# A gated graph layer in fp32: the pairwise-distance products in four row groups of TensorE, written ahead of the projection

## The chip, the core and the metric

The kernel runs on one core of a Trainium2 chip. A core has five engines, each with its own queue of instructions that it works through in order: TensorE (matrix products, in the profile PE, with its weight loads as PEld), VectorE (DVE), ScalarE (ACT), GpSimd (POOL) and SyncE (SP), which issues transfers. An engine waits for another through semaphores. SBUF is the working memory; TensorE writes its products to PSUM, which has eight banks, and VectorE or ScalarE reads them from there. The metric is the device time of one execution in microseconds. Three runs of the kernel before took 2278.29, 2275.20 and 2278.82 us; the median is 2278.29 us. The profile is of one further execution of 2278.09 us, whose span is 2276.3 us.

## The reference

There are 64 graphs of 256 nodes with 256 features each, all in fp32. Cut to what matters for one graph `x` with adjacency `adj`:

```
h      = relu(bn(conv1(x)))                  # 1x1 convolution
x_conv = relu(bn(conv2(h)) + x)              # 17 taps along the nodes
s      = x @ w_se.T + b_se                   # 256 nodes x 3 coordinates
dist   = |s_n|^2 + |s_m|^2 - 2 s_n . s_m     # 256 x 256
A      = exp(-dist) * adj
x_nmp  = A @ relu(x @ w_msg.T + b_msg)
r, z, n = GRU gates of ([x_conv, x_nmp], x)  # 512 -> 768 and 256 -> 768
x1     = layernorm(x + (1 - z) * n + z * x)
out    = layernorm(x1 + layer 1 of (x1, adj))
```

Layer 1 normalizes x1, aggregates it over `adj`, multiplies by two weights (W_rel, W_root), takes the relu, adds x1, and the result is normalized again. The change touches only how `dist` is computed and when. The matrix of distances is symmetric, and its rank is small: the product that makes it contracts over 4 values a node, three coordinates and a norm.

## The kernel before, in words

A graph's 256 nodes are two halves of 128, since SBUF and TensorE have 128 rows; `C` is 2. All products are fp32, which TensorE does in two passes, so that a product has two weight loads and two matmul records in the profile (transposes have one).

The main loop goes over 8 batches of 8 graphs. In iteration `k` it does, for different graphs at once, the stages of a software pipeline: the gates of graph `k` (`gates_rz`, `gates_n`, once for each half), the message passing of `k + 1` (`passing`), the factors and the distances of `k + 2` (`factors`, `distances`), the messages of `k + 3` (`messages`), and the projection and aggregation of `k - 1` (`transposes_h`, `project`, `aggregate`). Between the stages stand calls of `pump()`, each of which emits a slice of the convolution of the next batch. The convolution is done by a tree of splits on VectorE (the many instructions at L103, L302, L304, L361, L431 on the tile XF), products on TensorE (L384) and merges on VectorE. In the first part of a batch `pump()` instead emits conv1: transposes of x (L456), their copy by ScalarE (L457), the product (L465) and its activation (L481). The last batch has no convolution to prepare.

The order of the work on every engine is the order in which it is written (`manual_schedule`): nothing is moved by a planner. So where a stage is written sets what stands behind it on each of the engines.

The PSUM pool has eight banks under one tag. A bank comes back when the last reader of its tile has been written, and the banks are given out again in the order in which they came back. The first product into a bank waits until the earlier tile's reader has run.

The path of the distances of a graph, in the lines that the prediction speaks of:

- `messages` (L637): the product with the message weights also gives the 3 coordinates of a node. VectorE (L652) writes them into a tile `st`, twice, 32 columns apart (SR = 32), and GpSimd writes the norm beside each (L663). L654 adds the bias of the messages.
- `factors` (L667): TensorE transposes `st` (L671), so that the two copies come to rows 0 to 3 and 32 to 35 (ROWS = 36); ScalarE makes the two factors `lr` of it (L673, L674).
- `distances` (L677): one product for each half of the rows, 4 rows deep and 256 columns wide, each from its own copy: the products sit in two different groups of 32 rows of TensorE, and each has its own bank (L683). ScalarE takes Exp of both (L685), with the norm `ns` as bias.
- `mask` (L688): VectorE multiplies by the adjacency; `passing` (L695, L697) multiplies with the messages and copies the result.

Around it: `gates_rz` ends in L716 (VectorE adds the bias) and L717 (ScalarE, tanh); `gates_n` ends in L726 (VectorE), which frees its bank. `project` (L788) makes two banks, with a copy of each (L789). `update` is written in three steps: two VectorE instructions and a tanh (L739); then L743 and on, with the statistics (L730, L731) and GpSimd's power (L752 to L757); then L762 and L765. `aggregate` (L800, L802) reads the adjacency, and its result is written out after L816 and L817. `products` of the convolution takes three banks, which `take()` frees (L399 on ScalarE, L400 and L401 on VectorE).

In the iteration the part around the change is: `factors(k + 2)`, `gates_n(k, 1)`, `pump()`, `project(k - 1)`, `step(up)`, `pump()`, `distances(k + 2)`, `step(up)`, `pump()`, `messages(k + 3)`.

Of the kernel before, what the change touches and what calls it, by code (L numbers as in the profile page):

```python
# [12 lines left out]
F32 = mybir.dt.float32  # L13
AF = mybir.ActivationFunctionType
ALU = mybir.AluOpType

P = 128
B, N, D = 64, 256, 256
C = D // P
# [30 lines left out]
LEAVES += [(U + 4 + k, U + 6 + k, a) for k, a in enumerate(leaf_angles(PI / 2, 2))]  # L50
LEAVES += [(U + 2, U + 3, PI / 2)]
NM = 3 * len(LEAVES) + 2
SR, ROWS = 32, 36
OB = 7


# [19 lines left out]
def gnn_two_layers(  # L76
# [17 lines left out]
    nc = tc.nc  # L94
    const = ctx.enter_context(tc.tile_pool(name="const", bufs=1))
# [3 lines left out]
    def bank(name):  # L99
        return psum.tile([P, 512], F32, tag="ps", name=name)  # L100
# [514 lines left out]
    XG, ADJ, XT, NMP, AT, MSG, X1, H, ST, RZ, OUTS = ({} for _ in range(11))  # L615
# [21 lines left out]
    def messages(k, idle=False):  # L637

        MSG[k] = ahead.tile([P, C, D], F32, tag="msg", name="msg", bufs=3)
        st = sts[k % len(sts)]  # L640
        twice = st.rearrange("p m (r e) -> p m r e", e=SR)
        for m in range(C):
            ps = bank("ps_msg")
            for c in range(C):
                nc.tensor.matmul(ps[:, :D + 4], XT[k][:, c, m * P:(m + 1) * P], wms[:, c, :],  # L645
                                 start=(c == 0), stop=(c == C - 1 and not idle))
            if idle:
                nc.tensor.matmul(ps[:, :D + 4], ones[0:1, :], bms[0:1, :], start=False, stop=True)
                nc.scalar.copy(twice[:, m, :, 0:3], ps[:, D:D + 3].unsqueeze(1).to_broadcast([P, 2, 3]))
                nc.scalar.activation(MSG[k][:, m, :], ps[:, :D], AF.Relu)  # L650
                continue
            nc.vector.tensor_add(twice[:, m, :, 0:3], ps[:, D:D + 3].unsqueeze(1).to_broadcast([P, 2, 3]),  # L652
                                 bms[:, D:D + 3].unsqueeze(1).to_broadcast([P, 2, 3]))
            nc.vector.tensor_add(MSG[k][:, m, :], ps[:, :D], bms[:, :D])  # L654
        if not idle:
            nc.scalar.activation(MSG[k], MSG[k], AF.Relu)  # L656

        sq = ahead.tile([P, C, 3], F32, tag="sq", name="sq", bufs=2)
        ns = ahead.tile([P, C], F32, tag="ns", name="ns", bufs=3)
        nc.gpsimd.tensor_mul(sq, st[:, :, 0:3], st[:, :, 0:3])  # L660
        nc.gpsimd.tensor_add(ns, sq[:, :, 0], sq[:, :, 1])
        nc.gpsimd.tensor_add(ns, ns, sq[:, :, 2])
        nc.gpsimd.tensor_scalar(twice[:, :, :, 3], ns.unsqueeze(2).to_broadcast([P, C, 2]), -0.5, None, ALU.mult)  # L663
        nc.gpsimd.tensor_scalar(ns, ns, -1.0, None, ALU.mult)
        ST[k] = (st, ns)

# [10 lines left out]
    def distances(k):  # L677
        lr, ns = ST[k]
        AT[k] = ahead.tile([P, C, N], F32, tag="AT", name="AT", bufs=2)
        pss = [bank("ps_dist") for _ in range(C)]  # L680
        for m in range(C):
            r = slice(m * SR, m * SR + 4)
            nc.tensor.matmul(pss[m][:, :N], lr[r, 0, m * P:(m + 1) * P], lr[r, 1, :], start=True, stop=True)  # L683
        for m in range(C):
            nc.scalar.activation(AT[k][:, m, :], pss[m][:, :N], AF.Exp, bias=ns[:, m:m + 1], scale=2.0)  # L685

    def mask(k):
        nc.vector.tensor_mul(AT[k], AT[k], ADJ[k])  # L688
# [232 lines left out]
    with tc.tile_pool(name="filters", bufs=1, side="right") as filter_pool:  # L921
        FIRST["taps"] = filter_pool.tile([TAPS * OB, NM * OB], F32, name="taps")
        nc.scalar.dma_start(out=FIRST["taps"], in_=tb_dram.ap())
        fl = filters(filter_pool)
        next(first)
        next(fl)
        batch_norms()

        next(first)
        along_rows(filter_pool, 1, bn2_row)  # L930
        next(fl)
        places = 0
        for t in first:
            places += t is None
            if places == 5:
                break

        done, groups = 0.0, 0

        def filter_steps(last):  # L940
            nonlocal done, groups
            while groups < last:
                next(fl)
                groups += 1
                while done < 40.0 * groups / 19 and 0 not in STAGE:
                    done += next(first) or 0.0

        filter_steps(15)

        lone = const.tile([ROWS, 2], F32)  # L950
        ab = np.zeros((ROWS, 2), np.float32)
        for r in range(0, ROWS, SR):
            ab[r:r + 3, 0] = 1.0
            ab[r + 3, 1] = 1.0
        nc.sync.dma_start(out=lone, in_=nc.inline_tensor(ab, name="last_row_one").ap())

        sts = [const.tile([P, C, 2 * SR], F32, name=f"st{i}") for i in range(3)]
        for st in sts:
            nc.gpsimd.memset(st, 0.0)

        wms = const.tile([P, C, D + 4], F32)
        nc.vector.memset(wms[:, :, D + 3:], 0.0)
        nc.sync.dma_start(out=wms[:, :, :D], in_=wmsgT.rearrange("(c p) n -> p c n", p=P))
        nc.sync.dma_start(out=wms[:, :, D:D + 3], in_=wseT.rearrange("(c p) n -> p c n", p=P))
        bms = const.tile([P, D + 4], F32)
        nc.vector.memset(bms[:, D + 3:], 0.0)
        nc.sync.dma_start(out=bms[:, D:D + 3], in_=bse.rearrange("r o -> o r").to_broadcast([P, 3]))
        nc.sync.dma_start(out=bms[:, :D], in_=rows[:, R_MSG:R_MSG + D].to_broadcast([P, D]))
        brel = const.tile([P, D], F32)
        nc.sync.dma_start(out=brel, in_=rows[:, R_REL:R_REL + D].to_broadcast([P, D]))  # L970

        brzn = const.tile([P, 4 * D], F32)
        nc.sync.dma_start(out=brzn[:, :3 * D], in_=rows[:, R_IH:R_IH + 3 * D].to_broadcast([P, 3 * D]))
        nc.sync.dma_start(out=brzn[:, 3 * D:], in_=rows[:, R_HH + 2 * D:R_HH + 3 * D].to_broadcast([P, D]))
        gb = const.tile([P, 2, C], F32)
        nc.sync.dma_start(out=gb, in_=rows[:, R_GAMMA:R_GAMMA + 2 * D].rearrange("o (v c p) -> p (o v) c", p=P, c=C))
        whh = weight(whhT, D, 3 * D, "whh", nc.sync)

        wrr = const.tile([P, C, 2 * D], F32)
        nc.sync.dma_start(out=wrr[:, :, :D], in_=wrel.rearrange("(c p) n -> p c n", p=P))  # L980
        nc.sync.dma_start(out=wrr[:, :, D:], in_=wroot.rearrange("(c p) n -> p c n", p=P))

        store_w2(0)
        filter_steps(20)
        for _ in fl:
            pass
# [24 lines left out]
    for k in range(3):  # L1011
        load_adj(k)
    wih = weight(wihT, 2 * D, 3 * D, "wih", nc.sync, work)
    bhh = work.tile([P, 2 * D], F32, name="bhh", bufs=1)
    nc.sync.dma_start(out=bhh, in_=rows[:, R_HH:R_HH + 2 * D].to_broadcast([P, 2 * D]))
    nc.gpsimd.tensor_add(brzn[:, :2 * D], brzn[:, :2 * D], bhh)
    load_x(0)
# [10 lines left out]
    for b in range(NB):  # L1028
        coming = conv(b + 1) if b + 1 < NB else iter(())
        done, at, goal = 0.0, 0, BG * POINTS - 6  # L1030

        def pump():
            nonlocal done, at
            at += 1
            while done < CONV_WEIGHT * at / goal:
                t = next(coming, 1e9)
                if t is None:
                    break
                done += t

        for k in range(b * BG, min((b + 1) * BG, B - 1)):
            load(k + 3)
            load_x(k + 1)
            up = update(k)
            agg = None
            gates_rz(k, 0)
            pump()
            gates_n(k, 0)
            step(y_left)
            pump()  # L1050
            if k > 0:
                transposes_h(k - 1)
            pump()
            gates_rz(k, 1)
            pump()
            if k + 1 < B:
                passing(k + 1)
            pump()
            if k + 2 < B:
                factors(k + 2)  # L1060
            gates_n(k, 1)
            pump()
            if k > 0:
                project(k - 1)
            step(up)
            pump()
            if k + 2 < B:
                distances(k + 2)
            step(up)
            pump()  # L1070
            if k + 3 < B:
                messages(k + 3)
            step(up)
            pump()
            if k + 2 < B:
                mask(k + 2)
            if k > 0:
                agg = aggregate(k - 1)
            step(agg)
            step(agg)  # L1080
            pump()
            y_left = agg
        for _ in coming:
            pass
# [44 lines left out]
```

## Time and profile before

| | busy us | share of the span |
|---|---|---|
| TensorE, matmul | 2224.9 | 98% |
| TensorE, weight load | 1462.4 | 64% |
| VectorE | 1679.6 | 74% |
| ScalarE | 766.7 | 34% |
| GpSimd | 470.1 | 21% |

| group | count | mean ns |
|---|---|---|
| L683 matmul of the distances, 4 rows, 256 columns | 256 records | 426 |
| L685 Exp, 128x256 | 128 | 465 |
| L788 projection, 512 columns | 504 records | 592 |
| L384 conv product, 256 columns | 1316 records | 385 |

The profile's timeline has a row for a run of equal instructions: the start in us from the start of the span, the time to the end of the last of them, engine, line, operation, tiles (out <- in), shape, count, and in brackets the idle time of the engine just before and what ended it. Matmuls overlap in their records: one with 512 columns is recorded with 592 ns, while the next starts 430 ns later. So TensorE's real pace is read from starts, and its losses from the idle times, not from busy time. The view of waits has a row for each pair of who waited and for whom: total us, times, longest. The chain of work goes back from the last instruction, at each step to what released it; its shares say on which engine the end of the program hangs.

### The profile page before, as it was taken

Reading aid. Unit: us, or ns where it says so; the run is one execution under the profiler, and the core shown is the slowest. Engines: PE = TensorE matmul, PEld = TensorE weight load, DVE = VectorE, ACT = ScalarE, POOL = GpSimd, SP = SyncE. Lnnn points to the kernel's source line nnn. Section 1 sums busy time; section 2 is a strip of 40 time slices with the busy share of each in tenths; the row PEclk is TensorE's granted clock in tenths of the full one; section 3 lists DMA queues with packets and bytes.
Section 4 is the critical chain, followed back from the end, with each engine's and each line's share of the span. In section 5 each row is a group of like instructions: output and inputs, shape, how many; then the busy total and the mean of one; then the engine's idle time right before and its main releaser. Section 6 shows DMA issues by size and latency. Waiting matters only on the chain.

```text
span 2276.3 us, 24486 instructions
## 1 busy us (share of the span) xinstructions
PE 2224.9 (98%) x8386; PEld 1462.4 (64%) x8386; DVE 1679.6 (74%) x3194; ACT 766.7 (34%) x1588; POOL 470.1 (21%) x935
## 2 busy tenths in 40 slices
PE   8999999999999999999999999999999999999997
PEld 5775666666666676656666666666666566666664
DVE  6966889388883998749896698938889298874444
ACT  6433222532234322443224322343213532243332
POOL 0101222122120321223122121222122022121211
PEclk9999999999999999999999999999999999999998
DMA  5931433214422152223422143221442315321100
GB/s 147 314 112 65 139 102 97 97 47 134 139 75 98 58 166 87 75 102 110 144 75 95 63 138 112 85 101 52 139 134 74 102 37 167 101 79 37 47 23 14
DMA packets 212681, 226.68 MB, mean 100 GB/s; under 512 B 22103, under 2 KB 203854, under 8 KB 212558
## 3 DMA queue, kind: packets, MB, share of 16 engines
q1 hardware_dynamic: 190128, 191.27, 26.6%
q10 hardware_dynamic: 22430, 33.86, 4.3%
q8 instruction: 67, 1.10, 0.2%
q14 instruction: 56, 0.46, 0.1%
HBM read 179.22 MB, written 45.88 MB: 99 GB/s over the span
## 4 chain that ended last, share of the span: by engine, by line
PE 77%; DVE 15%; DMA 2%; issue 2%; POOL 1%; ACT 1%; SPq 0%; ACTq 0%; POOLq 0%; DVEq 0%
PE ps_rz L713 16%; PE ps_k L384 11%; PE ps_rz L711 8%; PE ps_n L725 8%; PE ps_out L788 6%; DVE XF L103 5%; PE ps_c L465 5%; PE ps_nmp L695 4%; PE ps_n L723 4%; PE ps_msg L645 4%; PE ps_out L800 4%; DMA w<-w2m 2%; PE ps_w L229 2%; DVE w L103 1%; DVE bst L730 1%
## 5 line engine op out<-in xcount | busy, mean ns | idle before, releaser
L103 DVE SCALAR_TENSOR_TENSOR XF<-XF 128x512 f32<-128x512 f32 (+2 forms) x800 | 507.9, 666 | 7.4
L752 POOL TENSOR_SCALAR q<-mv 128x2 f32<-128x2 f32 x63 | 31.9, 506 | 1452.7 <-DVE mv L731 1452.7
L384 PE MATMUL ps_k<-w,XF 128*128 128x256 f32 x1316 | 301.9, 385 | 14.9 <-ACT AT L685 11.6
L384 PEld LDWEIGHTS ps_k<-w,XF 128*128 128x128 f32 x1316 | 248.6, 192 | 63.1 <-ACT AT L685 17.3
L726 DVE TENSOR_TENSOR gn<-ps_n,brzn 128x512 f32<-128x512 f32 x128 | 88.1, 688 | 236.8 <-PE ps_n L725 236.8
L717 ACT ACTIVATE rz<-rz 128x512 f32<-128x512 f32 x128 | 80.6, 630 | 509.3 <-DVE rz L716 509.3
L711 PE MATMUL ps_rz<-whh,xT 128*128 128x512 f32 x512 | 240.9, 593 | 0.0
L713 PE MATMUL ps_rz<-wih,xc 128*128 128x512 f32 x512 | 240.6, 592 | 0.0
L713 PE MATMUL ps_rz<-wih,nmp 128*128 128x512 f32 x512 | 240.6, 592 | 0.0
L716 DVE TENSOR_TENSOR rz<-ps_rz,brzn 128x512 f32<-128x512 f32 x128 | 87.2, 681 | 189.5 <-PE ps_rz L713 189.5
L788 PE MATMUL ps_out<-wrr,hT 128*128 128x512 f32 x504 | 226.6, 592 | 0.0
L713 PEld LDWEIGHTS ps_rz<-wih,nmp 128*128 128x128 f32 x512 | 97.3, 190 | 122.5 <-issue 122.5
L713 PEld LDWEIGHTS ps_rz<-wih,xc 128*128 128x128 f32 x512 | 97.3, 190 | 122.4 <-issue 122.2
L788 PEld LDWEIGHTS ps_out<-wrr,hT 128*128 128x128 f32 x504 | 95.7, 190 | 96.2 <-issue 86.3
L656 ACT ACTIVATE msg<-msg 128x512 f32<-128x512 f32 x61 | 38.4, 630 | 334.2 <-DVE msg L654 334.2
L645 PE MATMUL ps_msg<-wms,xT 128*128 128x260 f32 x512 | 131.6, 395 | 4.4 <-DVE XF L400 4.4
L711 PEld LDWEIGHTS ps_rz<-whh,xT 128*128 128x128 f32 x512 | 92.2, 190 | 64.8 <-issue 61.2
L723 PE MATMUL ps_n<-whh,xT 128*128 128x256 f32 x512 | 131.6, 379 | 0.0
L725 PE MATMUL ps_n<-wih,xc 128*128 128x256 f32 x512 | 131.4, 379 | 0.0
L725 PE MATMUL ps_n<-wih,nmp 128*128 128x256 f32 x512 | 131.4, 379 | 0.0
L361 DVE TENSOR_TENSOR XF<-XF 128x512 f32<-128x512 f32 (+3 forms) x128 | 126.1, 1011 | 1.7
L465 PE MATMUL ps_c<-xTc,w 128*128 128x512 f32 x256 | 117.0, 600 | 6.1 <-ACT xTc L457 6.1
(139 smaller groups left out, 3503.0 us busy)
## 6 DMA issues: line engine op xcount, KB each, us to landing
w<-w2m SPq DMA_DIRECT2D x105, 768.0 KB, 6.1
xn<-in_x_dram SPq DMA_DIRECT2D x32, 512.0 KB, 4.4
xt<-xTc ACTq DMA_DIRECT2D x32, 512.0 KB, 3.2
xT<-xt SPq DMA_DIRECT2D x64, 256.0 KB, 3.0
xb<-in_x_dram SPq DMA_DIRECT2D x32, 512.0 KB, 6.0
adj<-in_adjT_dram SPq DMA_DIRECT2D x64, 256.0 KB, 2.8
x<-in_x_dram SPq DMA_DIRECT2D x64, 256.0 KB, 3.0
out_dram<-y ACTq DMA_DIRECT2D x63, 256.0 KB, 2.2
```

Of the source, the lines that this page charges most:

```text
L103: nc.vector.scalar_tensor_tensor(o, in0, s, in1, op0=op0, op1=op1)
L361: (nc.vector.tensor_add if add else nc.vector.tensor_sub)(sl(o, n), sl(a, n), sl(b, n))
L384: nc.tensor.matmul(ps, X[:, slot, c * P:(c + 1) * P], w(m, c), start=(c == 0), stop=(c == C - 1))
L465: nc.tensor.matmul(pss[o], w1[:, c, o * P:(o + 1) * P], xTc[:, c, :], start=(c == 0), stop=(c == C - 1))
L645: nc.tensor.matmul(ps[:, :D + 4], XT[k][:, c, m * P:(m + 1) * P], wms[:, c, :], start=(c == 0), stop=(c == C - 1 and not idle))
L695: nc.tensor.matmul(ps[:, d * N:(d + 1) * N], MSG[k][:, m, d * P:(d + 1) * P], AT[k][:, m, :], start=(m == 0), stop=(m == C - 1))
L711: nc.tensor.matmul(prz, XT[k][:, c, q], whh[:, c, 0:2 * D], start=(c == 0), stop=False)
L713: nc.tensor.matmul(prz, t, wih[:, i, 0:2 * D], start=False, stop=(i == 3))
L723: nc.tensor.matmul(pn[:, D:], XT[k][:, c, q], whh[:, c, 2 * D:], start=(c == 0), stop=(c == C - 1))
L725: nc.tensor.matmul(pn[:, :D], t, wih[:, i, 2 * D:], start=(i == 0), stop=(i == 3))
L788: nc.tensor.matmul(ps, hT[:, c, n * P:(n + 1) * P], wrr[:, c, :], start=(c == 0), stop=(c == C - 1))
L800: nc.tensor.matmul(po, ADJ[k][:, m, n * P:(n + 1) * P], hr[:, m, :], start=False, stop=(m == C - 1), skip_group_check=True)
```

## The change

The distance products are cut in four quarters of 128x128, for each half of the rows and each half of the columns. `st` gets four copies of the coordinates and norms in place of two, 32 columns apart, so that after the transposes (now 100 columns) each quarter has its own copy in its own group of 32 rows of TensorE, and its own bank. The four products can so stand in TensorE side by side. There are four Exp of 128 columns each in place of two of 256. The stage is written right after `gates_n(k, 1)`, ahead of `pump()`, of `project(k - 1)` and of the tanh in the first step of `update`, in place of after them: Exp then stands ahead of that tanh and of the projection's copies in ScalarE's queue, and the banks of the distances come back before the convolution's products ask for banks. The room in SBUF for the larger `st` comes from `bhh`, which is used once at the start and now shares the buffer of `hr`.

```diff
-SR, ROWS = 32, 36
+SR, ROWS = 32, 100
...
-        pss = [bank("ps_dist") for _ in range(C)]
+        pss = [[bank("ps_dist") for _ in range(C)] for _ in range(C)]
         for m in range(C):
-            r = slice(m * SR, m * SR + 4)
-            nc.tensor.matmul(pss[m][:, :N], lr[r, 0, m * P:(m + 1) * P], lr[r, 1, :], start=True, stop=True)
+            for n in range(C):
+                i = (m * C + n) * SR
+                nc.tensor.matmul(pss[m][n][:, :P], lr[i:i + 4, 0, m * P:(m + 1) * P], lr[i:i + 4, 1, n * P:(n + 1) * P],
+                                 start=True, stop=True)
         for m in range(C):
-            nc.scalar.activation(AT[k][:, m, :], pss[m][:, :N], AF.Exp, bias=ns[:, m:m + 1], scale=2.0)
+            for n in range(C):
+                nc.scalar.activation(AT[k][:, m, n * P:(n + 1) * P], pss[m][n][:, :P], AF.Exp, bias=ns[:, m:m + 1],
+                                     scale=2.0)
...
-    bhh = work.tile([P, 2 * D], F32, name="bhh", bufs=1)
+    bhh = work.tile([P, C, D], F32, tag="hr", name="bhh", bufs=1).rearrange("p c d -> p (c d)")
...
             gates_n(k, 1)
+            if k + 2 < B:
+                distances(k + 2)
             pump()
             if k > 0:
                 project(k - 1)
             step(up)
             pump()
-            if k + 2 < B:
-                distances(k + 2)
             step(up)
```

The other changed lines follow from it: the broadcasts of L652 and L663 (and of L649 for the first three graphs) write four copies in place of two, and the tiles `st` are 4 x 32 columns wide.

More of the change, by code (lines that the diff above doesn't have):

```diff
@@ L640, in messages @@
         st = sts[k % len(sts)]
-        twice = st.rearrange("p m (r e) -> p m r e", e=SR)
+        copies = st.rearrange("p m (r e) -> p m r e", e=SR)
         for m in range(C):
@@ L648, in messages @@
                 nc.tensor.matmul(ps[:, :D + 4], ones[0:1, :], bms[0:1, :], start=False, stop=True)
-                nc.scalar.copy(twice[:, m, :, 0:3], ps[:, D:D + 3].unsqueeze(1).to_broadcast([P, 2, 3]))
+                nc.scalar.copy(copies[:, m, :, 0:3], ps[:, D:D + 3].unsqueeze(1).to_broadcast([P, 4, 3]))
                 nc.scalar.activation(MSG[k][:, m, :], ps[:, :D], AF.Relu)
                 continue
-            nc.vector.tensor_add(twice[:, m, :, 0:3], ps[:, D:D + 3].unsqueeze(1).to_broadcast([P, 2, 3]),
-                                 bms[:, D:D + 3].unsqueeze(1).to_broadcast([P, 2, 3]))
+            nc.vector.tensor_add(copies[:, m, :, 0:3], ps[:, D:D + 3].unsqueeze(1).to_broadcast([P, 4, 3]),
+                                 bms[:, D:D + 3].unsqueeze(1).to_broadcast([P, 4, 3]))
             nc.vector.tensor_add(MSG[k][:, m, :], ps[:, :D], bms[:, :D])
@@ L662, in messages @@
         nc.gpsimd.tensor_add(ns, ns, sq[:, :, 2])
-        nc.gpsimd.tensor_scalar(twice[:, :, :, 3], ns.unsqueeze(2).to_broadcast([P, C, 2]), -0.5, None, ALU.mult)
+        nc.gpsimd.tensor_scalar(copies[:, :, :, 3], ns.unsqueeze(2).to_broadcast([P, C, 4]), -0.5, None, ALU.mult)
         nc.gpsimd.tensor_scalar(ns, ns, -1.0, None, ALU.mult)
@@ L955, in gnn_two_layers @@
         nc.sync.dma_start(out=lone, in_=nc.inline_tensor(ab, name="last_row_one").ap())
-        sts = [const.tile([P, C, 2 * SR], F32, name=f"st{i}") for i in range(3)]
+        sts = [const.tile([P, C, 4 * SR], F32, name=f"st{i}") for i in range(3)]
         for st in sts:
```

## The prediction

> **What bounds the kernel now.** I read the page first, then TensorE's waits, then the timeline of one period. The loop repeats every eight graphs; I name a graph by the one whose distances are computed, and take graphs 23 to 30 (908 to 1143 us).
>
> ```profile
> PE 2224.9 (98%) x8386; PEld 1462.4 (64%) x8386; DVE 1679.6 (74%) x3194; ACT 766.7 (34%) x1588; POOL 470.1 (21%) x935
> PE 77%; DVE 15%; DMA 2%; issue 2%; POOL 1%; ACT 1%; SPq 0%; ACTq 0%; POOLq 0%; DVEq 0%
> ```
>
> TensorE is nearly full, but 15% of the chain of work lies on VectorE: where the two hand over decides what a faster TensorE is worth. TensorE's own waits:
>
> ```profile
> PE ps_k L384 <- ACT AT L685: 11.6, 14, 1.1
> PE ps_c L465 <- ACT xTc L457: 6.1, 10, 0.8
> PE ps_msg L645 <- DVE XF L400: 4.4, 12, 0.5
> ```
>
> The first line is what the edit aims at: conv products (L384) wait for a bank that Exp (L685) still holds, 14 times, always in the two graphs of a period that are 29 and 30 here. Graph 29 in order of time:
>
> ```profile
> 1097.50 1.88 PE L788 MATMUL ps_out<-wrr,hT 128*128 128x512 f32 x4
> 1099.31 0.70 PE L683 MATMUL ps_dist<-lr 4*128 4x256 f32 x4
> 1099.94 1.13 PE L384 MATMUL ps_k<-w,XF 128*128 128x256 f32 x4
> ...
> 1102.20 4.58 PE L384 MATMUL ps_k<-w,XF 128*128 128x256 f32 x20 [1.12 <-ACT AT L685]
> ...
> 1107.14 0.68 DVE L400 TENSOR_TENSOR XF<-XF,ps_k 128x512 f32<-128x512 f32 x1
> ...
> 1107.87 1.15 PE L645 MATMUL ps_msg<-wms,xT 128*128 128x260 f32 x4 [0.22 <-DVE XF L400]
> ```
>
> To see: after the 1.12 us wait TensorE still comes 0.22 us too early for the bank that L400 frees. Two more stretches, graph 28 and graph 25:
>
> ```profile
> 1053.77 1.03 PE L725 MATMUL ps_n<-wih,nmp 128*128 128x256 f32 x4
> 1054.51 0.63 ACT L717 ACTIVATE rz<-rz 128x512 f32<-128x512 f32 x1 [1.53 <-DVE rz L716]
> 1054.63 3.60 PE L788 MATMUL ps_out<-wrr,hT 128*128 128x512 f32 x8
> 1055.97 0.35 ACT L674 COPY lr<-ps_sT 36x256 f32<-36x256 f32 x1
> 1058.16 0.70 PE L683 MATMUL ps_dist<-lr 4*128 4x256 f32 x4
> ```
>
> ```profile
> 959.73 3.60 PE L788 MATMUL ps_out<-wrr,hT 128*128 128x512 f32 x8
> 963.36 0.37 ACT L789 COPY hr<-ps_out 128x256 f32<-128x256 f32 x1 [1.34 <-PE ps_out L788]
> 963.63 0.63 ACT L739 ACTIVATE nn<-nn 128x512 f32<-128x512 f32 x1
> 964.30 0.69 DVE L743 TENSOR_TENSOR w<-x,nn 128x512 f32<-128x512 f32 x1 [2.15 <-ACT nn L739]
> 977.27 1.13 PE L465 MATMUL ps_c<-xTc,w 128*128 128x512 f32 x2 [0.58 <-ACT xTc L457]
> ```
>
> To see in 28: the factors lr are complete at 1056.32, but gates_n ends at 1054.63; only the projection (3.43 us) between them hides that. To see in 25: the tanh L739 runs behind the second copy L789, so it starts when the projection ends, and the chain from it ends in a wait of TensorE.
>
> **What the Trainium skill says.** "TensorEngine Tiling (Array Packing)", Tiling Modes: a change of tiling mode drains the array. The trace agrees: the distances' weight load has 0.76 us of idle before it where its neighbours have 0.24, and the load after them 0.33. "TensorE: Matmul & The Clock Gate", Part 3 (measured speedup): matmuls in different row groups run together, about 4 ns apart, so a pack lasts about one matmul. The trace shows this for two groups (four records within 0.70 us), none for four. Same page, specification table: ScalarE and VectorE are strict FIFO; the row of L739 agrees. "ScalarE: Activation LUTs", What ACT_TABLE_LOAD costs: about 280 ns plus 0.833 ns an element with a pointer bias, 93 ns of it overlapped. For 256 elements that is 493 ns; the trace has 465 and decides.
>
> **The change, part by part.**
>
> 1. *Four quarters.* Now: the four projection records of 1097.50 step by 0.43, so ordinary work could go on at 1099.22. L384 starts at 1099.94, and its four records take 1.13 where undisturbed ones (L725) take 1.03. The block costs 0.72 + 0.10 = 0.82 us a graph. Both passes shrink from 256 to 128 columns: 512 columns take 0.43, so 128 take 0.107, and 2 x 0.107 = 0.21 is saved, less two more groups' start, some 0.02 by the page: **0.19 us**; the drains stay. Bounds: 0 saved or worse if four groups don't overlap (four blocks of two passes, 8 x 0.107 = 0.86 of streaming against 0.21), 0.21 if they do so perfectly. I take 0.19; new block 0.63.
>
> 2. *Four Exp of 128 columns.* Two take 0.82; by the page's price four take about 3 x 0.29 + 0.36 = 1.2. ScalarE (34%) has the room: behind them stand the copies L789, which wait for the projection's 3.43 us anyway. The wider broadcasts of L652 and L663 (6 more values a row), the 100-column transposes (under a 128-column stream), the taller lr and the moved bhh cost nothing: each lies beside a longer neighbour.
>
> 3. *Exp ahead of the tanh.* The 14 bank waits go: 11.6 + 14 x 0.10 for the restart = 13.0 us. But between gates_n's end and L400 in graph 29 VectorE has no gap: from 1096.0 to 1107.8 it is busy 11.46 of 11.80 us, in 30 11.22 of 11.50. It begins with gn (L726), which follows gates_n as before; so L400 stays where it is, and TensorE waits longer at L645. **Gain in graphs 29 and 30: 0**, the 0.19 included. A bank goes out in the order in which banks came back; with four taken for the distances, the projection's first becomes that of gates_n, which gn frees at 1096.68. TensorE gets there at 1095.79 + 0.63 = 1096.42: some 0.3 us of a new wait, also inside that slack (1.12 + 0.10 + 0.22 + 0.19 = 1.6 us).
>
> 4. *The wait for lr.* In graph 28 the distances come at 1054.63, lr at 1056.32: 1.69 us late; in 27 (1030.38 against 1029.03) 1.35, in 24 (930.67 against 930.62) 0.05; the other five are 0.26 to 1.57 early. TensorE runs in order, so the projection and all behind it stand still meanwhile. A landing adds 0.06 (Exp ends at 1102.14, L384 starts at 1102.20), and 0.09 of the drain, the time from the end of the projection's stream at 1099.22 to the load at 1099.31, overlaps. What makes lr late is VectorE's backlog (rz L716, then L717, L697, L673, L674), 24.03 busy of the 25.3 us from 1004.3.
>
> 5. *That backlog starts later.* In graph 26 it starts with L431 at 1004.29, after 1.89 us of idle, released by L481, the copy of the conv1 products that follow gates_n (L465 at 999.99). The distances now stand ahead of them: +0.63, and VectorE's only pause from there to lr, 0.93 us at L762, is a part of its own chain through GpSimd. Graph 27: TensorE is 0.19 earlier (26's gain), lr 0.63 later: wait 1.35 - 0.03 + 0.19 + 0.63 = **2.14**. TensorE is then 2.14 - 0.38 = 1.76 later; graph 28: 1.69 - 0.03 + 0.63 - 1.76 = **0.53**. Net of 26 to 28: 2.14 + 0.53 - 3 x 0.19 = **+2.10 us**; VectorE had 3.79 us of idle ahead of graph 29's gn, so TensorE's lateness passes on. Without the shift by 0.63 it would be 1.5.
>
> 6. *Graph 25.* Its distances ran after the projection, inside the wait at L465; now they push the projection's end, hence L739 and with it the chain of L743, the statistics, GpSimd's power, L816 and L457 up to L465, by **+0.63** (six periods have this wait).
>
> 7. *Graphs 23 and 24*: -0.19 each, but 24's lr, late by 0.05 and VectorE's, gives 0.21 back: **-0.17**.
>
> Sum: 7 periods x 2.10 = 14.7, the first some 0.7 milder (lr late by 0.99 and 1.33): 14.0; 6 x 0.63 = 3.8; 7 x -0.17 = -1.2; the last seven graphs, TensorE without waits, 7 x -0.19 = -1.3. **+15.3 us: 2293.5.** Without the shift of step 5 it is 7 x 0.6 less, +11; with the waits of 27 and 28 longer by 0.3 each, +19.
>
> **The rivals.**
> - *Faster, 2253:* the bank waits were real and lr comes in time: -13.0 - 64 x 0.19 = -25. For it: they are TensorE's largest wait. Against: L400 in the third fence, lr in the fourth. 8%.
> - *No change, 2278:* lr waits come (7 x 2.7 + 1.4 = 20) with graph 25's 5, but L400 moves up with Exp, since its copy L399 stood behind it: 20 + 5 - 25 = 0. Against: L400 comes 4 us after that copy. 11%.
> - *Much slower, 2320:* four row groups in turn: 0.86 - 0.21 = 0.65 more where the block is on the path (five of eight graphs in seven periods and the last seven, 42), +27 on the forecast. For it: no trace shows four. Against: the two row groups of now overlap. 7%.
>
> **How the numbers follow.** Forecast 74%. It and the third rival are slower (81%); the second lies within 0.2% with 9 of its 11, 1 on each side; faster 9%, same 9%, slower 82%. The range goes from the second rival, 2277, to the forecast with larger waits, 2303, and leaves out the first, the third and tails.
>
> **What would show it.** Right: a new wait of L683 on ACT lr L674, about 20 us in 14 to 21 pieces, up to 2.1; no wait of L384 on L685; the wait of L645 on L400 up from 4.4 to about 15; L465's longest in a period up from 0.58 to about 1.4; the distances' records within some 0.5 us. Wrong: L645's wait unchanged with L685's gone (step 3), no wait for lr (step 4), or the records of L683 in a row (step 1).

## The result, and the profile after

The changed kernel takes **2297.6 us** (median of six runs, 2296.36 to 2302.11) against 2277.57 us of the kernel before on the same chip (six runs, 2275.20 to 2279.92): a ratio of **1.0091** [1.0078, 1.0104], 0.9% slower. The forecast was 2293.5 us, in a range from 2277 to 2303. The span of the profiled execution grew by 18.8 us, from 2276.3 to 2295.1, against the forecast's 15.3.

In the changed file some lines have other numbers: the product of the distances is L685 (L683 before), Exp is L689 (L685 before), gates_n's product L730 and its addition L731, the projection L793, its copy L794, the tanh of the update L744. L384 to L481, L645 and L671 to L674 are where they were.

First the page's busy times and the share of each engine in the chain of work:

```profile
PE 2218.3 (97%) x8642; PEld 1468.0 (64%) x8642; DVE 1680.0 (73%) x3194; ACT 791.4 (34%) x1716; POOL 463.9 (20%) x935
PE 64%; DVE 27%; issue 3%; POOL 3%; ACT 2%; DMA 1%; ACTq 0%; SPq 0%; POOLq 0%; DVEq 0%
```

TensorE is busy for less time (2218.3 us instead of 2224.9) in a longer span. The share of VectorE in the chain went from 15% to 27%: more of what the end of the program hangs on is VectorE's work. Then TensorE's waits (sum, number, longest, us):

```profile
PE ps_msg L645 <- DVE XF L400: 15.9, 14, 1.3
PE ps_dist L685 <- ACT lr L674: 13.8, 9, 2.1
PE ps_c L465 <- ACT xTc L457: 12.0, 10, 2.2
PE ps_out L793 <- ACT AT L689: 6.1, 14, 0.4
```

The wait for Exp's bank that stood first (L384, 11.6 us) is gone. In its place stands the first line, L645 on L400, up from 4.4: the same 14 places, paid a few instructions later. The second line is new, and the third has doubled. The timeline of graph 29 shows the exchange, where before there was the 1.12 us wait of L384:

```profile
1106.28 0.50 PE L685 MATMUL ps_dist<-lr 4*128 4x128 f32 x8
1107.22 3.70 PE L793 MATMUL ps_out<-wrr,hT 128*128 128x512 f32 x8 [0.44 <-ACT AT L689]
1110.76 5.34 PE L384 MATMUL ps_k<-w,XF 128*128 128x256 f32 x24
...
1117.54 0.68 DVE L400 TENSOR_TENSOR XF<-XF,ps_k 128x512 f32<-128x512 f32 x1
...
1118.27 0.93 PE L645 MATMUL ps_msg<-wms,xT 128*128 128x260 f32 x3 [1.29 <-DVE XF L400]
```

All 24 conv records now run without a break, and TensorE then stands 1.29 us at L645, since L400 is VectorE's and did not move up. In graph 27 the distances stand at the front of TensorE's queue, and lr is late:

```profile
1035.12 1.03 PE L730 MATMUL ps_n<-wih,nmp 128*128 128x256 f32 x4
...
1037.80 0.37 ACT L674 COPY lr<-ps_sT 100x256 f32<-100x256 f32 x1
1038.22 0.50 PE L685 MATMUL ps_dist<-lr 4*128 4x128 f32 x8 [2.08 <-ACT lr L674]
1038.65 5.40 PE L793 MATMUL ps_out<-wrr,hT 128*128 128x512 f32 x8
1038.74 1.14 ACT L689 ACTIVATE AT<-ps_dist,ns 128x128 f32<-128x128 f32 x4 [0.57 <-PE ps_dist L685]
```

To see: the wait of 2.08 us (2.14 was forecast); the eight records of the four quarters within 0.50 us; and a thing that was not forecast: the projection takes 5.40 us where it takes 3.60 or 3.70 elsewhere. The same place by stretches (length, then busy time and count of TensorE, its weight loads, VectorE, ScalarE, GpSimd; then the granted clock, the DMA share and GB/s) says why:

```profile
1033.23:1036.64 3.41, 2.92 (x15) 2.25 (x13) 3.38 (x5) 2.30 (x5) 0.00 (x0) 1.00 0.41 134
1036.64:1040.05 3.41, 1.83 (x12) 0.99 (x13) 3.34 (x5) 2.67 (x8) 0.00 (x0) 1.00 0.06 20
1040.05:1043.47 3.42, 3.42 (x6) 1.35 (x5) 3.35 (x6) 0.37 (x1) 0.00 (x0) 0.50 0.00 0
```

The stretch that holds the wait has TensorE busy for 1.83 of 3.41 us; in the next stretch of 3.41 us TensorE was granted half its clock (0.50), which costs 3.41 / 2 = 1.7 us of work. This followed the wait in three of the six periods that have it (windows at 1040.1, 1313.1 and 1589.6 us).

**Where the 18.8 us came from,** by the starts of the same records in both traces ("window" means a step of 3.41 us at half clock): graphs 26 to 28 of all periods but the first +16.0 (three periods of 2.08 and three, those with a half-clock window, of 3.25: so the windows are 3 x 1.17 = 3.5 of it); graph 25 +3.3; the first period +3.1; the tail +1.5, by one more half-clock window; graphs 23 and 24, with shorter waits for a weight, -2.3; graphs 29 and 30, with a window that only the kernel before had, -1.7; the last seven graphs -1.2. The sum is 18.7.

### The profile page after: what moved, and what is told of

It reads as the page before. It is cut to its first block, busy times and chain, and to the rows that moved or that the text cites. A ratio compares the mean times of both kernels' runs of the same rounds, so it can differ in the third digit from the quotient of the medians.

```text
span 2295.1 us, 25017 instructions
## 1 busy us (share of the span) xinstructions
PE 2218.3 (97%) x8642; PEld 1468.0 (64%) x8642; DVE 1680.0 (73%) x3194; ACT 791.4 (34%) x1716; POOL 463.9 (20%) x935
## 4 chain that ended last, share of the span: by engine, by line
PE 64%; DVE 27%; issue 3%; POOL 3%; ACT 2%; DMA 1%; ACTq 0%; SPq 0%; POOLq 0%; DVEq 0%
PE ps_rz L718 12%; PE ps_k L384 10%; DVE XF L103 9%; PE ps_rz L716 6%; PE ps_n L730 6%; PE ps_out L793 5%; PE ps_c L465 5%; PE ps_nmp L700 3%; PE ps_n L728 3%; PE ps_out L805 3%; PE ps_msg L645 2%; DVE w L103 2%; DVE bst L735 2%; DVE XF L431 2%; PE ps_w L229 2%
## 5 line engine op out<-in xcount | busy, mean ns | idle before, releaser
L384 PE MATMUL ps_k<-w,XF 128*128 128x256 f32 x1316 | 293.8, 380 | 2.1 <-DMA w<-w2m 0.8
L384 PEld LDWEIGHTS ps_k<-w,XF 128*128 128x128 f32 x1316 | 248.4, 190 | 47.6 <-issue 8.2
L731 DVE TENSOR_TENSOR gn<-ps_n,brzn 128x512 f32<-128x512 f32 x128 | 87.9, 687 | 224.1 <-PE ps_n L730 224.1
L793 PE MATMUL ps_out<-wrr,hT 128*128 128x512 f32 x504 | 239.1, 618 | 6.1 <-ACT AT L689 6.1
L793 PEld LDWEIGHTS ps_out<-wrr,hT 128*128 128x128 f32 x504 | 93.5, 194 | 111.2 <-issue 96.9
L645 PE MATMUL ps_msg<-wms,xT 128*128 128x260 f32 x512 | 127.2, 386 | 15.9 <-DVE XF L400 15.9
L645 PEld LDWEIGHTS ps_msg<-wms,xT 128*128 128x128 f32 x512 | 95.9, 190 | 56.5 <-issue 23.5
L730 PE MATMUL ps_n<-wih,xc 128*128 128x256 f32 x512 | 131.4, 379 | 0.0
L730 PE MATMUL ps_n<-wih,nmp 128*128 128x256 f32 x512 | 131.4, 379 | 0.0
L465 PE MATMUL ps_c<-xTc,w 128*128 128x512 f32 x256 | 116.8, 599 | 12.0 <-ACT xTc L457 12.0
```

The lines of the kernel that those rows point to most:

```text
L384: nc.tensor.matmul(ps, X[:, slot, c * P:(c + 1) * P], w(m, c), start=(c == 0), stop=(c == C - 1))
L465: nc.tensor.matmul(pss[o], w1[:, c, o * P:(o + 1) * P], xTc[:, c, :], start=(c == 0), stop=(c == C - 1))
L730: nc.tensor.matmul(pn[:, :D], t, wih[:, i, 2 * D:], start=(i == 0), stop=(i == 3))
L731: nc.vector.tensor_add(RZ[k][1][:, n, :], pn, brzn[:, 2 * D:])
L793: nc.tensor.matmul(ps, hT[:, c, n * P:(n + 1) * P], wrr[:, c, :], start=(c == 0), stop=(c == C - 1))
```

## The experiments

The theory was the prediction's: the four quarters save 0.19 us a graph, but their place ahead of the projection turns lr's lateness and VectorE's backlog into waits of TensorE, and the bank waits that it removes were hidden by L400. The chief rival was that the quarters themselves cost more than they save. Each run is compared with the kernel before on the same chip, which took 2277.38, 2278.61 and 2278.28 us in the three groups of runs (e1 to e4, e5 to e8, e9). The change itself was not run again beside them: where a run is set against its 2297.6 us, a microsecond or so may be the chips'. In the edits below the guards (`if k + 2 < B:` and the like) are mostly left out, and several calls stand on one line.

**e1: the quarters at the old place.** The change with the call moved back:

```
 gates_n(k, 1)
-distances(k + 2)
 pump(); project(k - 1); step(up); pump()
+distances(k + 2)
 step(up)
```

> The four quarters alone, at the old place behind the projection and the tanh. Theory of the place (the loss comes from where the distances stand; the quarters themselves save 0.19 us of TensorE wherever the block is on the path: five graphs in each of seven periods and the last seven, 42 in all): 42 x 0.19 = 8 us faster than before, about 2269.5. Rival, the banks and ScalarE (four banks and four Exp are what costs): slower than before, 2281 or more.

Measured: 2297.61 us, ratio 1.0084 [1.0067, 1.0100], 28 us above the theory's number. A miss. Its waits and its graph 29:

```profile
PE ps_dist L685 <- ACT AT L689: 27.8, 14, 2.3
```

```profile
1109.48 0.50 PE L685 MATMUL ps_dist<-lr 4*128 4x128 f32 x6
...
1111.31 0.63 ACT L744 ACTIVATE nn<-nn 128x512 f32<-128x512 f32 x1 [1.36 <-DVE nn L103]
1111.85 0.86 ACT L689 ACTIVATE AT<-ps_dist,ns 128x128 f32<-128x128 f32 x3
1112.25 0.79 PE L685 MATMUL ps_dist<-lr 4*128 4x128 f32 x2 [2.28 <-ACT AT L689]
```

Three quarters run (six records), and the fourth (two) waits 2.28 us for the Exp of one of the first. At that place three of the eight banks are held by conv products and two by the projection; three are free and four are wanted. The Exp that gives one back stands behind a tanh (L744), which waits for VectorE. This happens in graphs 29 and 30 alone (2.28 and 1.70 us; a half-clock window follows in all seven periods behind the first and in five behind the second). In the others the quarters saved 0.20 us each, but for graph 25, where the wait at L465 hides it. So the quarters were not slow, but a fourth bank was wanted where none was free, and the new place does have a use: it is where four banks are free in these two graphs. The count of banks is read from the order of the code; e5 and e6 test it.

**e2: the new place alone.** The two halves of before, written ahead of the projection:

```
 gates_n(k, 1)
+distances(k + 2)      # two products of 256 columns, two banks
 pump(); project(k - 1); step(up); pump()
-distances(k + 2)
```

> The move alone, with the two halves of before. Theory of the place: all the waits of the change come, and the block is 0.83 in place of 0.63, so 7 to 10 us slower than the change, about 2305. Rival, the banks and ScalarE: without four banks and four Exp the loss is mostly gone, 2290 or less.

Measured: 2307.17 us, 1.0129 [1.0111, 1.0147]; 2305 was expected.

```profile
PE ps_msg L645 <- DVE XF L400: 20.2, 14, 1.6
PE ps_dist L683 <- ACT lr L674: 12.6, 7, 2.1
PE ps_c L465 <- ACT xTc L457: 11.7, 10, 1.9
```

The three waits of the change are there without the quarters, so they belong to the place. With the quarters the kernel is 9.6 us faster (2297.6).

**e3: the factors earlier, too.** The change, with `factors(k + 2)` moved ahead of `gates_rz(k, 1)`:

```
+factors(k + 2)
 gates_rz(k, 1); pump(); passing(k + 1); pump()
-factors(k + 2)
 gates_n(k, 1)
```

> The change with the factors written ahead of the second half's gates, so that lr does not stand behind the tanh that waits for VectorE. Theory of the place: the waits of the distances for lr go, and with them the half clock behind the long one: 12.5 + 2.4 + 5 = 20 us faster than the change, about 2277 (2273 to 2280); what is left of the loss is the projection pushed back in one graph of eight, six times 0.55, against the 8 us of the quarters. Rival, the banks and ScalarE: no more than 5 us faster than the change, 2292 or more.

Measured: 2285.11 us, 1.0036 [1.0023, 1.0048]: 12.5 below the change, where 20 were expected. The waits for lr and the half-clock windows in the loop are gone, but another has come:

```profile
PE ps_sT L671 <- POOL st L663: 11.1, 7, 3.5
```

The transposes now come too early for GpSimd's norm: 1.27 us in each of six periods and 3.5 in the first. By the starts of the same records, graph 27 takes 2.10 us less than in the change, or 3.80 where the window was, and graph 26 takes 1.48 more. Half right: lr's lateness cost what was said, and the cure has a price of its own.

**e4: only graphs 29 and 30, with halves.** The kernel before, with the distances ahead of the tanh in these two graphs alone, but still behind the projection:

```
 pump(); project(k - 1)
+early_exp = k % BG in (3, 4)
+if early_exp:
+    distances(k + 2)
 step(up); pump()            # step(up) holds the tanh
-if k + 2 < B:
+if k + 2 < B and not early_exp:
     distances(k + 2)
```

> The kernel before, with the distances ahead of the tanh (but still behind the projection) only in the two graphs of eight whose conv products wait for a bank that Exp holds. Theory (that wait is hidden: VectorE has no gap up to L400, on which TensorE waits next): no change, 2277.5 within 1.5; the wait of L384 on L685 gone, that of L645 on L400 up from 4.4 to about 16. Rival, the bank wait was real: 13 us faster, about 2264.5.

Measured: 2276.69 us, 0.9997 [0.9990, 1.0003]. The largest wait of the kernel before is taken away, 11.6 us of it, and the time stays: L384 waits no more for Exp, and L645 waits 1.60 and 1.28 us for L400 instead. So it is enough that Exp stands ahead of the tanh; the place ahead of the projection is not needed for that.

**e5 and e6: the quarters where they cost nothing.** In e5 all distances are at the old place, as halves in graphs 29 and 30 and as quarters elsewhere. In e6 all are quarters, ahead of the projection in these two and at the old place elsewhere:

```
 gates_n(k, 1)
-distances(k + 2)
+ahead_of_it = k % BG in (3, 4) and k < B - BG
+if ahead_of_it:
+    distances(k + 2)
 pump(); project(k - 1); step(up); pump()
+if k + 2 < B and not ahead_of_it:
+    distances(k + 2)
```

> The four quarters at the old place, but the two halves in the two graphs of eight (29 and 30 in a period) where only three banks are free there. Theory of the place and the free banks (the first run lost because the fourth quarter there took the bank of the first and waited for its Exp; elsewhere each quarter block saves 0.19): 42 x 0.19 = 8 us faster than before, about 2269.5, no wait of the distances on Exp. Rival, four banks or four Exp cost in every graph: no faster than before, 2277 or more.

> The four quarters everywhere, ahead of the projection only in the two graphs of eight whose conv products wait for banks, at the old place in the six others. Theory of the place: VectorE hides the two, the others save 0.19 where they are on the path: about 2269.5, the same as with the halves in the two. Rival (being ahead costs in every graph): 2275 or more.

Measured: e5 2267.81 us, 0.9951 [0.9937, 0.9965]; e6 2267.09 us, **0.9948** [0.9934, 0.9962]. Both beat both kernels, by 11 us against before and 30 against the change. Some 8 us against before were expected of the quarters; where the other 3 come from was not traced. The page of e6 and its largest waits:

```profile
PE 2205.7 (97%) x8642; PEld 1464.9 (65%) x8642; DVE 1679.7 (74%) x3194; ACT 787.5 (35%) x1716; POOL 471.9 (21%) x935
PE 81%; DVE 13%; DMA 2%; issue 2%; POOL 1%; ACT 1%; SPq 0%; ACTq 0%; POOLq 0%; DVEq 0%
```

```profile
PE ps_msg L645 <- DVE XF L400: 15.9, 14, 1.3
PE ps_c L465 <- ACT xTc L457: 8.2, 10, 1.9
```

No wait of L685 is left, VectorE is back to 13% of the chain, and the wait at L645 is as large as in the change, which shows once more that it is not what makes the change slow.

**e7: the array kept at work during the wait.** The change, with eight products that nobody reads, ahead of the distances of graph 27 in the six middle periods:

```
 gates_n(k, 1)
+if k % BG == 1 and BG < k < B - BG:
+    keep = bank("ps_warm")
+    for _ in range(8):
+        nc.tensor.matmul(keep[:, :P], ones, ones, start=True, stop=True)
 distances(k + 2)
```

> The change with eight products of a constant that nothing reads, put ahead of the distances in the graph with the wait of 2.1 us for lr (six of the seven periods), so that TensorE works through that wait: 1.7 us of work in it. Theory (the half clock that follows that wait in some periods comes from TensorE standing still): no window of half clock there, each one that goes is worth 1.7 less 0.46 for the next graph's wait, 3 of them in the profile of the change: 4 us faster than the change, about 2293.5. Rival (the half clock has another cause): the windows stay, the same time as the change or up to 1 us slower.

Measured: 2294.61 us (2291.74 to 2299.08), 1.0068 [1.0052, 1.0084], 3.0 below the change; the two kernels' runs overlap, so the times alone don't settle it. The trace does:

```profile
1040.24 1.95 PE L1070 MATMUL ps_warm<-ones 128*128 128x128 f32 x16
1042.50 0.50 PE L685 MATMUL ps_dist<-lr 4*128 4x128 f32 x8 [0.31 <-ACT lr L674]
1042.93 3.70 PE L793 MATMUL ps_out<-wrr,hT 128*128 128x512 f32 x8
```

The wait is filled, lr is as late as it was, and the projection takes 3.70 us again: there is no half-clock window behind this wait in any period. Nor is that owed to where the steps of the clock fell: in four of the six periods 1.75 us or more of the filled stretch lie within one step of 3.41 us, in two of them the whole 2.1 us, and in the change the three windows followed 1.58, 1.84 and 2.08 us of wait within one step.

**e8: four quarters in one row group.** The change with `i = 0` for all four quarters, so that all use the first copy:

```
-i = (m * C + n) * SR
+i = 0
```

> The change with all four quarters taken from the first copy, so all in the same row group of TensorE. Theory (the four quarters overlap only because they stand in four row groups): eight passes of 0.107 in a row, the block 0.63 longer, on the path in some 42 graphs: 26 us slower than the change, about 2324. Rival (banks alone let them overlap): 2300 or less.

Measured: 2329.89 us, 1.0231 [1.0206, 1.0256].

```profile
1510.42 1.15 PE L685 MATMUL ps_dist<-lr 4*128 4x128 f32 x8
1511.50 0.70 PE L793 MATMUL ps_out<-wrr,hT 128*128 128x512 f32 x1
```

The passes stand in a row, 0.11 us each: 1.08 us from the first to the projection (1511.50 - 1510.42), against 0.43 in the change (1038.65 - 1038.22 above). The third rival's 0.65 us a block is real when the groups don't run together, and absent in the change. The 6 us above the expectation go with half-clock windows: graph 27 has them in six of six periods here, two steps long in three, and in three of six in the change, one step long. (The trace is of the slowest of the four runs, 2340.87 us, so it may show more of them than the median run had.)

**e9: in graph 26 conv1 first.** The change, but for `k % 8 == 0` the distances stand behind the conv1 products, still ahead of the projection:

```
 gates_n(k, 1)
-distances(k + 2)
+if k % BG != 0:
+    distances(k + 2)
 pump()                 # the conv1 products, L465
+if k % BG == 0:
+    distances(k + 2)
 project(k - 1)
```

> The change, but in the one graph of eight (26 in a period) in which conv1 products follow the gates the distances stand behind these products, still ahead of the projection. Theory (the distances delay those products by 0.63 us, so VectorE's backlog starts that much later and the next graph's factors lr come that much later): idle of VectorE ahead of the first fold back from 2.52 to about 1.9, the wait for lr of the next graph down from 2.08 to about 1.5, 0.6 a period, and fewer windows of half clock: 4 to 8 us faster than the change, about 2292. Rival (the wait for lr comes from TensorE being earlier alone, VectorE's start is no part of it): the wait stays within 0.2 of 2.08.

Measured: 2288.69 us, 1.0051 [1.0038, 1.0064], 9 below the change (5.6 were expected). The wait of graph 27 went from 2.08 to 1.46 us: by 0.62, the length of the block that no longer stands ahead of conv1. The half-clock windows behind it fell from three to one. Six times 0.62 and two times 1.17 make 6.1 of the 8.7 us by which the profiled span is shorter (2286.4 against 2295.1); the rest lies in the first period and the tail, and was not taken apart.

## Why the prediction was right, and where it was short

The direction, the mechanism and the place of each wait held; the sum was some 4 us short. By its steps:

1. **The quarters: right.** The block takes 0.53 us from the end of gates_n's stream to the next work, and that work starts 0.10 slower: 0.63, as forecast; the last seven graphs gain 0.20 each. e8 shows what four groups in turn would have cost. It agrees with what the Trainium skill says in "TensorE: Matmul & The Clock Gate", Part 3, on row groups that run together; the records of the four groups start 7 ns apart here, where the page has about 4.
2. **Four Exp: right.** 1.14 us against 1.2. They delay the projection's copies by nothing that a wait shows.
3. **No gain from the bank waits: right,** shown by e4: without them L645 waits 1.60 and 1.28 us, and the time is the same. From gates_n's records to L645 graphs 29 and 30 take 13.81 and 13.49 us in the change, and the same before, but for the two graphs with a half-clock window. One detail was wrong: the projection's new wait is for Exp (L689), 0.44 us, and not for gates_n's addition: the bank of the first quarter comes back before that one. It lies inside the slack all the same.
4. **The waits for lr: right.** The view of waits has 2.08 in graph 27, 0.46 in 28 and 0.15 in 24, counted from the modelled end of the last matmul; by starts, as the prediction counted, the distances are 2.15, 0.53 and 0.21 later than without a wait (forecast: 2.14, 0.53, 0.21). In the three periods with a half-clock window that of 28 is hidden by it.
5. **The backlog that starts later: right,** shown by e9. In graph 26 VectorE's L431 now starts after 2.52 us of idle instead of 1.89, so 0.63 later. Net of graphs 26 to 28: +2.08 in the periods without a half-clock window (+2.10).
6. **Graph 25: right.** The wait at L465 is 1.33 us instead of 0.58, the graph +0.55 (0.63).
7. **Graphs 23 and 24: right,** -0.18 (-0.17), without the waits for a weight.

**The term that was mis-sized** is the one for graphs 26 to 28, "7 periods x 2.10 = 14.7, the first some 0.7 milder": with the first period (+3.1 instead of 1.4) it measures 19.1 instead of 14.0. Three of the six other periods cost 3.25 instead of 2.10, since TensorE came out of the wait at half clock. The prediction priced a wait at its length and left out what it does to the clock. The first period was not milder: a wait for hT grew there from 2.64 to 3.46 us, and two steps at half clock (203.8 to 210.6 us), which the trace of before does not have there, begin in it. That the time still lies in the range is in part luck: its upper end was drawn for longer waits, which did not come, and the clock took up that room.

Why the same wait is followed by a half-clock window in three periods and not in the other three can be read from the trace. The granted clock changes only at steps of 3.413 us: the starts of the three windows are 80.0 and 81.0 such steps apart ((1313.1 - 1040.05) / 3.413 and (1589.6 - 1313.1) / 3.413). Cut the span at these steps. In the period of 1313 us the whole wait lies in one stretch, shown with the one after it; in that of 767 us it lies in two, shown with the one after them:

```profile
1309.71:1313.12 3.41, 1.33 (x13) 0.78 (x12) 3.34 (x5) 2.20 (x6) 0.00 (x0) 1.00 0.43 130
1313.12:1316.53 3.41, 3.41 (x5) 1.33 (x6) 3.38 (x6) 1.05 (x4) 0.00 (x0) 0.50 0.00 0
...
760.16:763.57 3.41, 2.72 (x14) 2.06 (x12) 3.38 (x4) 2.30 (x5) 0.00 (x0) 1.00 0.45 149
763.57:766.99 3.42, 2.03 (x12) 1.18 (x13) 3.35 (x5) 2.48 (x8) 0.00 (x0) 1.00 0.01 4
766.99:770.40 3.41, 3.41 (x12) 2.05 (x11) 3.34 (x6) 1.27 (x3) 0.00 (x0) 1.00 0.00 0
```

Where all or most of the wait falls into one step, TensorE is busy for 1.33 us of that step (1.58 and 1.83 in the other two such periods), and half clock follows. Where a step's end cuts the wait more evenly, each part is busy for 2.03 us or more, and none follows. So in the change one and the same wait costs 2.1 us or 3.25 by where it lies on this grid. The busy time of a step is not the whole rule, though: in e4 a step with 1.81 us, which holds the wait of 1.60 us for L400, is followed by one at full clock, and so are three more like it.

```profile
562.00:565.41 3.41, 1.81 (x9) 1.25 (x8) 3.31 (x11) 0.00 (x0) 2.08 (x5) 1.00 0.00 0
565.41:568.83 3.42, 3.42 (x14) 2.26 (x13) 3.39 (x12) 1.61 (x3) 2.90 (x6) 1.00 0.12 22
```

The rivals: *faster* fell in graph 29, as its fence said; *no change* fell because L400 did not move; *much slower* fell with the records of L685, 7 ns apart.

## What to carry to other kernels

Before a wait is removed, find the next thing that its engine will wait for: if that thing hangs on another engine's unbroken run of work, the wait moves and the time stays (e4: 11.6 us of waits removed, nothing gained). In an in-order queue a stage that is moved forward needs its inputs that much earlier and delays all that it overtakes; move it in the iterations that gain by it, and leave it where it was in the others (e6 against the change: 30 us). And packing products into more row groups, each with a bank of its own as here, wants as many free banks as products: count the banks at the place where they are written (e1: the fourth waited up to 2.28 us).

## What the runs showed of the hardware

- **A wait can cost more than its length, by its place on a grid.** In these traces TensorE's granted clock changes only at steps of 3.413 us. In the loop of the change a step with TensorE busy for 1.33 to 1.83 us was followed by one at half clock, 1.7 us lost, and steps with 2.02 us and more were not; waits of 1.1 to 2.1 us in otherwise full work can be enough for that. No threshold comes out of it. Over the loops of all eleven traces (230 to 2200 us of each span) every step at full clock with less than 1.8 us was followed by half clock, and none with more than 2.3 us was. In between both happen: four steps with 1.81 us in e4 were not followed; in e8, where the distances stand for 1.15 us on four rows, steps with 2.09 to 2.28 us were, and in the kernel before two of five with 2.29. Work on four rows may count for less: without the distances' products the steps that were followed have at most 1.73 us and the others at least 1.42, a narrower overlap; no run tests this alone. The Trainium skill, "TensorE: Matmul & The Clock Gate", Part 1 (what's actually happening), has a free-running window of 3413 ns, with which the traces agree, and lets the clock fall after an idle window of about 3.4 us; there they disagree, since windows with TensorE busy for 1.33 to 1.83 us were followed by half clock. Eight products that nobody reads, put into the wait, prevented it in all six periods (e7).
- **Products in four row groups ran side by side.** Eight fp32 passes of 128 columns in four groups took 0.43 us from the first to the next ordinary work; in one group they stood in a row and took 1.08 us (e8).
